# A Mamba and attention kernel: the convolution as four column strips over taps loaded from DRAM, residuals on TensorE, and 10 of 16 pairs on GpSimd

## The chip, the cores and the metric

The kernel runs on one core of a Trainium2 chip. The metric is the device time of one execution in microseconds; a time is the median of several runs. Besides that there is one profiled execution, with a record of every instruction on each engine: PE (TensorE), DVE (VectorE), ACT (ScalarE), POOL (GpSimd), and SP (SyncE), which only issues DMAs.

## The reference, cut to what matters

The input `x` is two images of 256 channels by 64 x 64 positions, that is 4096 tokens each, float32. Layer 0 is `x + mamba(groupnorm(x))`, layer 1 is `x + attention(groupnorm(x))`. The change lies in layer 0:

```python
yn = (y - mu) * lax.rsqrt(var + 1e-05) * gamma + beta        # layer norm over 256 channels
xz = yn @ W_in.T
xm, z = (xz[..., :DI], xz[..., DI:])                         # DI = 512
xc = lax.conv_general_dilated(xc, conv_w, ...)               # causal, 4 taps, each channel alone
u = jax.nn.silu(xc + conv_b[None, :, None]).transpose(0, 2, 1)
proj = u @ W_xp.T                                            # 16 + 16 + 16 columns
dt = jax.nn.softplus(proj[..., :R] @ W_dt.T + b_dt)
Bm = proj[..., R:R + N]
Cm = proj[..., R + N:]
def step(h, inp):                                            # over the 4096 tokens
    dA = jnp.exp(dt_t[:, :, None] * A)
    h = dA * h + (dt_t * u_t)[:, :, None] * B_t[:, None, :]
    return (h, jnp.einsum('bdn,bn->bd', h, C_t))
ym = (ys.transpose(1, 0, 2) + u * D) * jax.nn.silu(z)
y2 = ym @ W_out.T + yn
y3 = jax.nn.gelu(y2 @ W1.T + b1, approximate=False) @ W2.T + b2 + y2
```

Layer 1 is eight heads of softmax attention over the 4096 tokens of an image; the change doesn't touch its work.

## The kernel before, in words

`mamba_stage` does layer 0, `attention` layer 1, one after the other on the same core. Channels lie on the 128 partitions; tokens are cut into tiles of 512 (`T`), so there are 16 tiles, image 0's eight and then image 1's eight. For each tile there are three kinds of work:

- `front(i)` makes the layer norm, the convolution (`conv`, once for each of the `KD` = 4 blocks of 128 inner channels), the projection `W_xp`, and the softplus of `dt` (`softplus`, once a block). `dt` and `dt * u` are stored to DRAM, and the steps read them back four channels to a partition group, repeated (`load_rep`); B and C rows come back from DRAM broadcast over the partitions (`load_row`).
- `step(g)` is the recurrence. A tile has 32 steps: 4 channel blocks k, 4 groups of states, and two halves. A step has two exponentials on ACT (`da`, L853), a broadcast of B by PE into PSUM (`bn`), products with B, two scans on DVE (L869), and the product with C on POOL (L875, 1024 columns). Every second step, four matmuls with a 128 x 32 matrix of ones sum the states into four strips of 32 rows of `y` (L901). They need `bn`, `dtu_rep` and `dt_rep`; rings of five `h`, two `bn` and two `dbu` buffers lie between the engines.
- `back(i)` does `W_out`, the residual, the MLP with GELU, and the two last additions, takes the group-norm statistics and stores the tile. In image 1's time, `qkv` also makes image 0's queries, keys and values on PE.

A pair is two steps. `pooled(pair)` says whether the product of `dtu` with B for the pair's odd channels is made by POOL in one instruction (`both_times_b`, L864) or by DVE in two (`times_b(1)`, L860); the even channels are always DVE's.

The convolution before: PE projects a block into PSUM; ACT copies it behind three columns kept from the last tile (`xm`, L585 to L587, with `halo`); and PE adds up four matmuls, each with a diagonal matrix of one tap and with `xm` shifted by a column:

```python
matmul(pc.tile, [(taps[:, k, j, :], xm.tile[:, j : j + T]) for j in range(TAPS)])
```

An fp32 matmul shows as two records in the profile. The residuals before depend on the image. For image 0, PE adds them by matmuls with an identity matrix (L646, L684, L686) and ACT takes the sum out of PSUM (L660, L700). For image 1, DVE adds from PSUM (L663, L702).

The order of all this is written by a planner, `Plan`. Every `add(engine, due, cost, emit, reads, writes, tables, lands)` is one task. The planner runs a small model of the five engines with the stated costs; at each moment each engine takes, among the tasks that are ready, whose buffers are free and that are due no later than `HORIZON` after the oldest task not yet placed, the one with the lowest `due` (a task that needs another ACT table counts `SWITCH` later). Due times are in steps. The tasks are then emitted in that order, so each engine's instruction stream, SP's included, is fixed: an instruction that waits holds up all behind it on its engine. `front(i + 1)` is planned into the time of tile i's steps, `back(i)` into that of tile i + 1.

The prologue before the first scan holds loads of weights, the statistics of both images (`first`, L336 and L337), the group norm, and tile 0's whole front; image 1's tiles are loaded for their statistics into the `h` ring.

## Time and profile before

| | |
|---|---|
| Median of 3 runs | 4293.21 us (4290.18 to 4297.77) |
| Profiled execution | 4292.38 us, span 4290.6 us |
| PE busy | 4115.5 us, 96% |
| DVE busy | 3866.3 us, 90% |
| ACT busy | 3727.0 us, 87% |
| POOL busy | 3750.8 us, 87% |
| DMA | 389.58 MB, mean 91 GB/s |
| First and last scan | 81.5 and 1950.8 us |
| First matmul of attention | 1993.1 us |

A row of the groups of instructions reads: line, engine, operation, output from inputs by the program's names (PSUM tiles of the `mm` ring all show as `mm`), shapes, how many, then busy time and mean ns of one, then the idle time of the engine just ahead of them and what ended it. A row of the table of stretches reads: the stretch and its length, busy time (and instructions) of PE, PEld (weight loads), DVE, ACT and POOL, the granted TensorE clock, the share of DMA time and GB/s. A row of the timeline: start, length, engine, line and operation, count, and in brackets the idle time ahead. Busy PE time includes waits inside its pipeline, so it is an upper bound on its work.

### The profile page before, as it was taken

Reading aid. Unit: us, or ns where it says so; the run is one execution under the profiler, and the core shown is the slowest. Engines: PE = TensorE matmul, PEld = TensorE weight load, DVE = VectorE, ACT = ScalarE, POOL = GpSimd, SP = SyncE. Lnnn points to the kernel's source line nnn. Section 1 sums busy time; section 2 is a strip of 40 time slices with the busy share of each in tenths; the row PEclk is TensorE's granted clock in tenths of the full one; section 3 lists DMA queues with packets and bytes.
Section 4 is the critical chain, followed back from the end, with each engine's and each line's share of the span. In section 5 each row is a group of like instructions: output and inputs, shape, how many; then the busy total and the mean of one; then the engine's idle time right before and its main releaser. Section 6 shows DMA issues by size and latency. Waiting matters only on the chain.

```text
span 4290.6 us, 58937 instructions
## 1 busy us (share of the span) xinstructions
PE 4115.5 (96%) x21154; PEld 1799.6 (42%) x21154; DVE 3866.3 (90%) x3309; ACT 3727.0 (87%) x4982; POOL 3750.8 (87%) x1913
## 2 busy tenths in 40 slices
PE   6799999999999999988999999999999999999998
PEld 2233333333334333333444444444454444444443
DVE  5899999999999999995898989899858989898998
ACT  5789898998788888875999999999859999999997
POOL 3999999999899999994898888889728988888887
PEclk8899999999999999999999999999999999999999
DMA  6334333334444444447101040110182110401100
GB/s 212 107 114 130 117 115 123 128 128 133 150 146 160 162 141 140 143 166 167 33 18 28 18 106 18 28 30 21 50 253 54 32 28 18 106 22 25 29 21 9
DMA packets 172302, 389.58 MB, mean 91 GB/s; under 512 B 23392, under 2 KB 49760, under 8 KB 163808
## 3 DMA queue, kind: packets, MB, share of 16 engines
q1 hardware_dynamic: 171120, 383.37, 29.4%
q8 instruction: 168, 2.75, 0.3%
q10 hardware_dynamic: 880, 2.36, 0.3%
q14 instruction: 134, 1.10, 0.1%
HBM read 292.33 MB, written 93.32 MB: 90 GB/s over the span
## 4 chain that ended last, share of the span: by engine, by line
PE 79%; DVE 12%; ACT 4%; issue 3%; DMA 1%; POOL 1%; SPq 0%; DVEq 0%; POOLq 0%; ACTq 0%
PE s L1162 25%; PE po L1199 23%; PE mm L448 15%; DVE h L869 7%; PE mm L688 4%; PE y L901 4%; PE bn L448 2%; PE mm L647 2%; DVE bn L860 2%; ACT da L853 1%; PE s L1046 1%; PE y L899 1%; ACT L248 1%; PE sums_ps L1250 1%; PE mm L684 1%
## 5 line engine op out<-in xcount | busy, mean ns | idle before, releaser
L1184 DVE TENSOR_REDUCE chunk<-chunk 128x1024 f32<-128x4096 f32 x288 | 1269.8, 4409 | 176.4 <-ACT chunk L1175 174.7
L1232 POOL TENSOR_TENSOR acc_p<-acc_p,e 128x1024 f32<-128x1024 f32 x480 | 1167.3, 2432 | 124.1 <-ACT e L1175 99.4
L875 POOL TENSOR_TENSOR h<-h,c 128x1024 f32<-128x1024 f32 x512 | 1203.4, 2376 | 32.8 <-issue 15.7
L1175 ACT ACTIVATE e<-s 128x1024 f32<-128x1024 f32 x1056 | 1084.6, 1030 | 91.8 <-PE s L1162 56.7
L1162 PE MATMUL s<-q,k 128*128 128x512 f32 x4096 | 1155.8, 415 | 7.0 <-ACT chunk L1175 2.6
L1175 ACT ACTIVATE chunk<-s 128x1024 f32<-128x1024 f32 x992 | 1119.8, 1129 | 48.2 <-PE s L1162 22.9
L1199 PE MATMUL po<-chunk,v 128*32 128x512 f32 (+1 forms) x5248 | 1057.0, 521 | 0.0
L1199 PE MATMUL po<-e,v 128*32 128x512 f32 (+1 forms) x5504 | 1019.3, 500 | 1.5 <-ACT e L1175 1.5
L1162 PEld LDWEIGHTS s<-q,k 128*128 128x128 f32 x4096 | 714.3, 189 | 624.8 <-ACT e L1175 235.4
L853 ACT ACTIVATE da<-dt_rep,neg_a 128x512 f32<-128x512 f32 x1024 | 695.6, 702 | 105.8 <-DVE h L869 101.4
L1230 POOL TENSOR_TENSOR acc_p<-acc_p,e 128x512 f32<-128x512 f32 x480 | 621.8, 1295 | 94.7 <-ACT e L1175 64.8
L869 DVE TENSOR_TENSOR_SCAN h<-da,state,dbu 128x512 f32<-128x512 f32 x512 | 651.5, 1275 | 14.3 <-PE y L901 7.1
L869 DVE TENSOR_TENSOR_SCAN h<-da,state,bn 128x512 f32<-128x512 f32 x512 | 647.0, 1264 | 11.4 <-PE y L901 5.5
L864 POOL TENSOR_TENSOR dbu<-dtu_rep,b 128x1024 f32<-128x1024 f32 x176 | 417.8, 2374 | 17.0 <-issue 7.3
L448 PE MATMUL bn<-proj,pick 112*128 112x512 f32 x512 | 341.9, 669 | 87.9 <-DVE h L869 84.8
L248 ACT ACT_TABLE_LOAD x312 | 400.3, 1283 | 6.2 <-PEq L1502 0.7
L1199 PEld LDWEIGHTS po<-e,v 128*32 128x32 f32 x5504 | 251.8, 109 | 269.7 <-issue 104.4
L860 DVE TENSOR_TENSOR bn<-dtu_rep,bn 128x512 f32<-128x512 f32 x512 | 346.8, 680 | 16.8 <-PE bn L448 8.5
L1199 PEld LDWEIGHTS po<-chunk,v 128*32 128x32 f32 x5248 | 241.5, 108 | 250.7 <-issue 250.7
L1229 DVE TENSOR_TENSOR acc<-acc,e 128x512 f32<-128x512 f32 x448 | 309.6, 691 | 17.4 <-ACT chunk L1175 0.5
L901 PE MATMUL y<-h,sum 128*32 128x512 f32 x2048 | 302.0, 615 | 8.5 <-POOL h L875 8.3
L448 PE MATMUL mm<-yn,w_in 128*128 128x512 f32 x512 | 257.0, 627 | 8.2 <-ACT yn L538 3.6
(149 smaller groups left out, 4177.2 us busy)
## 6 DMA issues: line engine op xcount, KB each, us to landing
dt_rep<-dt_dram SPq DMA_DIRECT2D x128, 512.0 KB, 5.0
dtu_rep<-dtu_dram SPq DMA_DIRECT2D x128, 512.0 KB, 5.3
k<-qk_dram SPq DMA_DIRECT2D x62, 512.0 KB, 7.4
q<-qk_dram SPq DMA_DIRECT2D x124, 256.0 KB, 4.8
b<-bc_dram SPq DMA_DIRECT2D x64, 256.0 KB, 3.2
c<-bc_dram SPq DMA_DIRECT2D x64, 256.0 KB, 3.9
dt_dram<-dt SPq DMA_DIRECT2D x64, 256.0 KB, 2.2
dtu_dram<-lw SPq DMA_DIRECT2D x64, 256.0 KB, 3.7
```

Source lines behind the costliest of these rows:

```text
L248: self.nc.scalar.preload_act_table_set(self.TABLES[task.table])
L448: nc.tensor.matmul(out, lhsT=lhsT, rhs=rhs, start=(i == 0), stop=(i == len(pairs) - 1))
L853: nc.scalar.activation(da[j].tile, dt.tile[:, j, :], AF.Exp, scale=scale)
L869: nc.vector.tensor_tensor_scan(h.tile[:, j, :], da[j].tile, dbu, initial, ALU.mult, ALU.add)
L875: nc.gpsimd.tensor_tensor(h.tile, h.tile, rows_c.tile.unsqueeze(1).to_broadcast([P, 2, T]), ALU.mult)
L901: nc.tensor.matmul(y.tile[j * PQ : (j + 1) * PQ, :], lhsT=sum4, rhs=pair[j // 2].h.tile[:, j % 2, :], start=False, stop=(qd == NQ - 1),)
L1162: nc.tensor.matmul(ps[:, j, :], lhsT=keys[i // NT, kt][:, h, kj : kj + P], rhs=queries[i][:, h, :], start=True, stop=True)
L1175: nc.scalar.activation(e, todo[s].s[half], AF.Exp, scale=SCALE)
L1184: nc.vector.tensor_reduce(out, terms, AX.XY, ALU.add)
L1199: nc.tensor.matmul(tiles[i].po[h * D : (h + 1) * D, cols], lhsT=v[:, c, g * P + h * D : g * P + (h + 1) * D], rhs=todo[s].e[h // 2][:, h % ...
L1230: nc.gpsimd.tensor_add(acc_p[:, 1, :], acc_p[:, 1, :], eb[:, 1, :])
L1232: nc.gpsimd.tensor_add(acc_p, acc_p, eb)
```

## The change

Three things change in the Mamba stage, and with them the due times of nearly all tasks and `HORIZON` (28 to 32).

1. The convolution. The projected block is copied whole to `xm`, stored to a row in DRAM that holds the image's whole length with three zeros ahead (`rows_x`), and read back by four loads, one a tap j: the row shifted by j columns, 32 channels to a partition group, four groups of channels side by side. So partition 32 j + c of `xs` holds tap j of channel c of each group. Four matmuls then do the convolution, one for each group of 32 channels, with a 128 x 32 matrix that holds the taps, into four strips of 32 rows of one PSUM tile. The `halo` copies are gone; eight small stores zero the rows' first three columns. `xs` has one buffer; for tile 0 all blocks but k = 2 use the two `dtu_rep` buffers. `xm` has two buffers, not three.
2. The residuals of image 1 are made as those of image 0: identity matmuls on PE, eviction by ACT.
3. `pooled` gives POOL 10 of 16 pairs, not 11.

`range_t`, a small tile of the attention stage, is allocated after the Mamba stage. The attention stage's instructions are unchanged. Cut to its core (due times and the residual code of image 1 that merely goes are shortened):

```diff
-HORIZON = 28
+HORIZON = 32
...
-    r_xm = Ring(sc, [P, HALO + T], "xm", 3)
+    r_xm, r_xs = ring("xm", 2, pool=sc), ring("xs", 1, TAPS, pool=sc)
...
-        add("SP", due + 8, 0.8, load, [], [xt], lands=3.0)
+        add("SP", due + 2.5, 0.8, load, [], [xt], lands=3.0)
...
-    taps = wp.tile([P, KD, TAPS, P], F32, name="taps")
+    taps = wp.tile([P, KD, P // PQ, PQ], F32, name="taps")
     for k in range(KD):
-        for j in range(TAPS):
-            nc.vector.tensor_scalar_mul(taps[:, k, j, :], ident, conv_w[:, k, j : j + 1])
+        for g in range(P // PQ):
+            nc.vector.tensor_scalar_mul(taps[:, k, g, :], same, conv_w[:, k, g : g + 1])
...
-    halo = wp.tile([P, IMAGES, KD, HALO], F32, name="halo")
-    nc.vector.memset(halo, 0.0)
+    rows_x = [[dr.tile([P, HALO + L], F32, name="x_dram", bufs=IMAGES * KD) for _ in range(KD)] for _ in range(IMAGES)]
+    row_bufs = [[Buf(parts=NT) for _ in range(KD)] for _ in range(IMAGES)]
+    for x in itertools.chain(*rows_x):
+        nc.sync.dma_start(x[:, 0:HALO], state[:, 0, 0, 0, 0:HALO])
...
-        px, pc, xm = Buf(mm), Buf(mm), Buf(r_xm, 2)
-        h = halo_buf[b * KD + k]
+        px, pc, xm, xs = Buf(mm), Buf(mm), Buf(r_xm), Buf(r_dtur if d is tiles[0] and k != 2 else r_xs, TAPS)
+        at, row = t * T, row_bufs[b][k]
...
+        def store():
+            nc.sync.dma_start(rows_x[b][k][:, HALO + at : HALO + at + T], xm.tile)
+
+        def load(j):
+            src = rows_x[b][k][:, at + j : at + j + T].rearrange("(g c) t -> c g t", c=PQ)
+            nc.sync.dma_start(xs.tile[j * PQ : (j + 1) * PQ, :, :], src)
+
         def convolve():
-            matmul(pc.tile, [(taps[:, k, j, :], xm.tile[:, j : j + T]) for j in range(TAPS)])
+            for g in range(P // PQ):
+                matmul(pc.tile[g * PQ : (g + 1) * PQ, :], [(taps[:, k, g, :], xs.tile[:, g, :])])
...
-        add("ACT", due - 5, 0.15, lambda: nc.scalar.copy(xm.tile[:, 0:HALO], halo[:, b, k, :]), [h], [xm[0]])
-        add("ACT", due + 2, 0.49, lambda: nc.scalar.copy(xm.tile[:, HALO:], px.tile), [px], [xm[1]])
-        add("ACT", due + 4, 0.25, lambda: nc.scalar.copy(halo[:, b, k, :], xm.tile[:, T:]), [xm], [h])
-        add("PE", due + 4.5, 3.44, convolve, [xm], [pc, d.u[k]])
+        add("ACT", due + 2, 0.49, lambda: nc.scalar.copy(xm.tile, px.tile), [px], [xm])
+        add("SP", due + 7.5, 0.9, store, [xm], [row[t]], lands=2.0)
+        for j in range(0, TAPS, 2):
+            add("SP", due + 2, 1.7, lambda j=j: (load(j), load(j + 1)), [row[t], row[max(t - 1, 0)]], [xs[j], xs[j + 1]], lands=3.3)
+        add("PE", due + 4, 1.1, convolve, [xs], [pc, d.u[k]])
...
-                if k == 0 and b == 0:
+                if k == 0:
                     nc.tensor.matmul(po.tile, lhsT=ident, rhs=yn.tile[:, m, :], start=True, stop=False)
...
-            if b == 0:
-                keep = lambda m=m, po=po: nc.scalar.copy(yn.tile[:, m, :], po.tile)
-                add("ACT", due + 2 * m + 8.5, 0.49, keep, [po], [yn[m]])
-            else:
-                plus = lambda m=m, po=po: nc.vector.tensor_add(yn.tile[:, m, :], yn.tile[:, m, :], po.tile)
-                add("DVE", due + 2 * m - 1.5, 0.6, plus, [po], [yn[m]])
+            keep = lambda m=m, po=po: nc.scalar.copy(yn.tile[:, m, :], po.tile)
+            add("ACT", due + 2 * m + 7, 0.49, keep, [po], [yn[m]])
...
-                    if b == 0:
-                        nc.tensor.matmul(acc.tile, lhsT=ident, rhs=xt.tile[:, m, :], start=False, stop=False)
+                    nc.tensor.matmul(acc.tile, lhsT=ident, rhs=xt.tile[:, m, :], start=False, stop=False)
...
-                x = xt.tile[:, m, :]
-                if b == 0:
-                    nc.scalar.activation(x, acc.tile, AF.Identity, bias=b_2[:, m : m + 1])
-                else:
-                    nc.vector.scalar_tensor_tensor(x, acc.tile, b_2[:, m : m + 1], x, ALU.add, ALU.add)
+                nc.scalar.activation(xt.tile[:, m, :], acc.tile, AF.Identity, bias=b_2[:, m : m + 1])
...
-        return pair * 11 % 16 < 11
+        return pair * 10 % 16 < 10
...
-        add("SP", g - 5.5, 1.7, load, [src], [rep[at], rep[at + 1]], lands=3.3)
+        add("SP", g + 2.5, 1.7, load, [src], [rep[at], rep[at + 1]], lands=3.3)
...
-        add("DVE", g + 4, 0.6, lambda: times_b(0), [dtu[quarter]], [bn])
+        add("DVE", g + 12.5, 0.6, lambda: times_b(0), [dtu[quarter]], [bn])
         for j, dbu in ((1, dbu1[quarter // 2]), (0, bn)):
-            add("DVE", g + 5, 1.185, lambda j=j: scan(j), [da[j], dbu, state_buf[states[j]]], [h[j]])
+            add("DVE", g + 12.5, 1.185, lambda j=j: scan(j), [da[j], dbu, state_buf[states[j]]], [h[j]])
...
-    add("SP", -19.5, 2.4, load_late, [], [late_buf], lands=12.0)
+    add("SP", -22, 2.4, load_late, [], [late_buf], lands=12.0)
...
+    taps = given["L0_conv_conv_w"].reshape(-1, P // 32, 32, 4)
+    arrays["conv_taps"] = taps.transpose(3, 2, 0, 1).reshape(P, -1)
+    arrays["same"] = np.kron(np.ones((4, 1)), np.eye(32)).astype(np.float32)
```

## The prediction

> **What bounds the kernel now.** I read the table of stretches first, cut at tile boundaries: four whole tiles of the first image (from the first `L646` matmul of one tile to that of the fourth after it) and four of the second (by the first `L663` addition). Columns: length, then busy time of PE, PEld, DVE, ACT and POOL, granted clock, DMA share, GB/s.
>
> ```profile
> 439.27:899.82 460.55, 440.54 (x1394) 168.77 (x1393) 444.62 (x485) 414.98 (x717) 458.05 (x221) 1.00 0.39 124
> 1273.52:1742.84 469.32, 460.49 (x1490) 187.21 (x1489) 462.43 (x518) 414.41 (x725) 459.54 (x221) 1.00 0.46 155
> ```
>
> Per tile: image 0 takes 115.1 us, of which POOL is busy 114.5, DVE 111.2, ACT 103.7. Image 1 takes 117.3, with DVE 115.6, PE 115.1, POOL 114.9, ACT 103.6. So image 0 is POOL's, and in image 1 three engines are level. Attention (from about 1963 us) is not touched by the change; I carry it unchanged.
>
> Next, the groups of instructions by shape, for prices:
>
> ```profile
> L875 POOL TENSOR_TENSOR h<-h,c 128x1024 f32<-128x1024 f32 x512 | 1203.4, 2376 | 32.8 <-issue 15.7 <-ACT state L872 14.1 <-POOL h L875 2.3
> L864 POOL TENSOR_TENSOR dbu<-dtu_rep,b 128x1024 f32<-128x1024 f32 x176 | 417.8, 2374 | 17.0 <-issue 7.3 <-PE bn L448 4.6 <-DMA dtu_rep<-dtu_dram 2.3
> L860 DVE TENSOR_TENSOR dbu<-dtu_rep,bn 128x512 f32<-128x512 f32 x160 | 107.8, 675 | 9.3 <-PE bn L448 8.4
> L663 DVE TENSOR_TENSOR yn<-yn,mm 128x512 f32<-128x512 f32 x15 | 10.3, 686 | 3.1 <-PE mm L647 2.9
> L702 DVE SCALAR_TENSOR_TENSOR x_back<-mm,b,x_back 128x512 f32<-128x512 f32 x14 | 10.5, 747 | 2.6 <-PE mm L688 2.6
> ```
>
> Instructions overlap a little at their ends: four POOL products run 9.33 us back to back in the timeline, 2.33 each; the starts of consecutive DVE elementwise ones stand 0.60 apart. I use these net costs.
>
> The timeline then gives both forms of matmul, side by side, at full clock:
>
> ```profile
> 1300.00 1.07 PE L901 MATMUL y<-h,sum 128*32 128x512 f32 x8
> 1301.33 3.60 PE L448 MATMUL mm<-xm,taps 128*128 128x512 f32 x8
> ```
>
> Eight records (one fp32 matmul is two) take 0.99 us in the chain when they go to four column strips, and 3.44 (8 x 0.43) over the full width.
>
> Last, start and end: SP's timeline, PE's at the start, and PE after the last scan.
>
> ```profile
> 29.52 4.55 SPq L336 DMA_DIRECT2D h<-in_x  x5
> 40.24 3.08 SPq L336 DMA_DIRECT2D h<-in_x  x3
> ...
> 47.01 7.03 PE L448 MATMUL mm<-xm,taps 128*128 128x512 f32 x16
> 54.82 3.63 PE L448 MATMUL mm<-u,w_xp 128*48 128x512 f32 x8 [0.44 <-ACT u L582]
> ...
> 1962.74 14.08 PE L448 MATMUL mm<-yn,w 128*128 128x512 f32 x32
> 1976.66 1.02 PE L684 MATMUL mm<-yn,ident 128*128 128x512 f32 x2
> 1977.52 7.03 PE L688 MATMUL mm<-hid,w 128*128 128x512 f32 x16
> ```
>
> SP is still issuing bulk loads at 43.3; PE runs without a gap in the last tile's residual and MLP, up to attention's first matmul.
>
> **The skill.** The Trainium skill, TensorEngine Tiling (Array Packing), Theoretical Speedup, gives up to 4x for a side of 32; the two rows above agree (3.44 against 0.99, 3.5x). DMA: Bandwidth & Descriptors, Queues, rings and completion order, says that each DMA engine takes descriptors in ring order: a small store queues behind bulk loads issued before it. Loads of `h` in the first 50 us land after up to 12 us, median 6.7, which fits. SBUF — State Buffer, Who interferes with whom: a DVE instruction with two SBUF inputs blocks against a GpSimd one for its whole length. Here the 128x1 subtraction at 1085.18 lasts 5.59 us, until POOL falls idle at 1090.76. The operations that the change adds to DVE read PSUM and one SBUF tensor, so they don't meet this lock.
>
> **The change, part by part,** per tile unless said.
>
> 1. *Ten pairs of 16 on POOL.* POOL loses one `L864` product: -2.32. DVE gains two `L860` products: +1.2 to +1.35.
> 2. *Image 1's residuals.* DVE loses two `L663` and two `L702`: 2 x 0.60 + 2 x 0.67 = -2.55. PE gains four identity matmuls of 0.86: +3.44. ACT gains two copies (0.58) and two Identity evictions (0.68): +2.5.
> 3. *Convolution.* PE: 4 x (3.44 - 0.99) = -9.8. ACT loses eight copies of three columns (0.187): -1.5. SP gains 4 stores and 16 loads. At 0.33 (the row of `dt_dram`) and 0.33 to 0.53 (`b`) that is 6.6 to 9.8 us of issue, over the roughly 17 it has now. They move 20 x 256 KB = 5.2 MB: 124 GB/s becomes about 172 in image 0, 155 about 203 in image 1; DMA share from 0.39 and 0.46 to about 0.53 and 0.60. I count this as nothing in mid-stream: the convolution of the next tile is made while this one's 32 steps run, and `u` k=3 of it can't be written before this tile's k=2 begins (five `u` buffers), so a round trip of 6 to 9 us has a cover of tens of us. Without that cover it would cost 6 us four times a tile. The loads start at odd addresses; the worst I allow is a fifth more DMA time, still below 0.75 share.
>
> The sum: image 0 has POOL 112.2, DVE 112.4, PE 9.8 lighter. Image 1 has POOL 112.6, DVE 114.2 (115.6 - 2.55 + 1.2), PE 108.7, ACT 104.6. DVE becomes the bound everywhere, with POOL level in image 0. The busiest engine is at 99.5% of the period in image 0 today (one engine at the top) and 98.5% in image 1 (three near it). After, two near the top: I take 99%. Periods 113.5 and 115.4, gains 1.6 and 1.9. Ends: at 99.5% 2.1 and 2.5; at 98% 0.4 and 0.8. Times 8 tiles each: -13 and -15, together -28 (ends -10 and -37).
>
> 4. *Start.* The four convolutions now go through DRAM before `u` exists, and nothing else can run. Four `w_in` pairs end near 40, so a copy is ready from 36. But SP takes its queue in order, and the image-1 loads ahead of it stall for buffers to 40.24 and issue to 43.3. First store about 43.5, landing about 48 behind 1.5 MB; its four loads land about 52, then two to two and a half us for each further convolution: last one at 59, silu 60.5, against `w_xp` starting at 54.82 now. +6. Best case, with SP free at 36: last convolution at 50, -3. Worst, with the eight small stores that zero the halos (8 x 0.4 us of issue) ahead as well and full DMA engines: +12. The first scan starts at about 81 today and shifts by the same.
> 5. *End.* The last tile's four added identity matmuls lie on PE's gapless run after 1955: +3.4. Bounds 0 (if the first pair runs ahead of the last gate) to 4.
> 6. *Order.* Due times and HORIZON move everywhere; a common shift of an engine's due times changes no ranking on that engine. Priced at 0, bounds -10 (the stretch 1080 to 1120, where POOL idles 10.3 us of 40 around the group norm) to +10.
>
> Sum: -28 + 6 + 3.4 = about -19. The profiled execution took 4292.4 us, span 4290.6; its span goes to about 4272, its time to 4273.5, and the runs' median, 4293.2, lies 0.8 above that time: 4274.
>
> **The rivals.**
>
> *PE was the brake (more gain).* The chain of waits gives PE most of image 1 and half of image 0, and DVE waits on PE's `bn` and `y`. If the lighter PE lets DVE and POOL run at 99.5% (-37), the start costs only 2, and the image boundary recovers 5: about 4257. Against it: POOL at 99.5% of image 0 can't be explained by PE.
>
> *No change.* Two engines level at the top starve each other through five `h` and two `dbu` buffers: 98%, -10, and start plus tail give +9: 4292. For it: no stretch of this kernel shows two engines above 98.6%.
>
> *Slower: SP's queue.* Each convolution puts a wait for a store's landing (2.2 to 3.7 us in the rows of `dt_dram` and `dtu_dram`) at the head of SP's in-order queue; behind it stand the `dt_rep` and `dtu_rep` loads, for which ACT's exponentials and DVE's products wait. At 1 us of recurrence lost for each of the 60 convolutions after the first tile it is +60, less the 19: about 4334; at 0.5 us, 4304. It decides from 19/60, about 0.3 us per convolution. Against it: today DVE loses only 7.6 us to `dtu_rep` in the whole run, while SP already waits such landings out 84 times.
>
> *The convolution doesn't pack* (column strips don't overlap because each strip has its own weights): PE keeps 3.44, image 1's PE rises above 118 and binds: slower, but `y` also loads weights for every strip and packs. I give it 0.02, within the slower case.
>
> **How the numbers follow.** Forecast 0.50 (4262 to 4287), more gain 0.20 (4248 to 4262), no change 0.13 (4285 to 4300), slower 0.17 (above 4302, centred at 4312). The measurement tells about 0.2%, 8.6 us: faster means below 4284.6, slower above 4301.8. Faster: 0.47 + 0.20 + 0.01 = 0.68; same: 0.03 + 0.12 = 0.15; slower 0.17. The range leaves out half of the slower case and a little at the bottom: 4250 to 4306; the forecast's own is 4262 to 4287.
>
> **What would show it.** The convolution's matmuls take about 1 us for eight records; `L864` counts 160 and `L860` on `dbu` 192; no DVE row for image 1's residuals; tile periods near 113.5 and 115.4 with DVE the busiest; first scan near 87; PE's tail after the last gate 3.4 longer; DMA share near 0.53 and 0.60. Wrong if DVE waits show `dtu_rep` or ACT's show `dt_rep` for tens of us, if a period stays at 115 with DVE and POOL both under 98%, or if the first scan comes after 93.

## The result, and the profile after

The changed kernel takes 4336.1 us (median of 4 runs, 4332.2 to 4339.3) against 4292.8 for the kernel before on the same chip: a ratio of 1.0099, interval 1.0081 to 1.0116. It is slower by 1%, where I forecast 4274 and gave slower 0.17. The profiled execution has a span of 4337.5 us.

I divided both spans at the first `W_out` matmul of each tile, which stands once in every tile in both kernels. A tile's period is the time from one such matmul to the next. (The forecast's -28 us counted eight tiles of each image; the table has seven periods of image 0, so its column adds up to -17.)

| Stretch | Before | After | Difference | Predicted |
|---|---|---|---|---|
| span's start to tile 0's `W_out` | 209.8 | 251.9 | +42.1 | +6 |
| seven periods of image 0 | 807.7 (115.4 each) | 818.2 (116.9 each) | +10.6 | -11.2 (-1.6 each) |
| tile 7's `W_out` to tile 15's | 938.3 | 927.9 | -10.4 | -15.2 (-1.9 each) |
| tile 15's `W_out` to the end | 2334.8 | 2339.5 | +4.6 | +3.4 |
| span | 4290.6 | 4337.5 | +46.9 | -17 |

Two rows carry the miss: the start (36 us more than forecast) and image 0 (22 us more).

The engines' work came out as summed. This is the table of stretches of the changed kernel, four whole tiles of each image, with the same columns as before:

```profile
369.50:835.64 466.14, 417.60 (x1393) 153.13 (x1392) 445.60 (x493) 390.76 (x668) 450.53 (x217) 0.95 0.57 168
1310.08:1771.81 461.73, 440.52 (x1525) 172.80 (x1521) 456.42 (x510) 409.86 (x701) 450.50 (x218) 0.99 0.67 204
```

Per tile, image 0 has POOL 112.6 (forecast 112.2), DVE 111.4 (112.4), PE 104.4; image 1 has DVE 114.1 (114.2), POOL 112.6 (112.6), PE 110.1 (108.7). But image 0's tile takes 116.5 in this stretch, so no engine is above 96.7% of it. PE has 9.8 us a tile less to do by the sum, but its busy time fell only from 110.1 to 104.4: its granted clock is 0.95 here, where it was 1.00. DMA share is 0.57 and 0.67 where I had 0.53 and 0.60.

The groups of instructions of the changed kernel show the parts themselves (lines have moved: `L876` is the product with C, `L865` and `L861` are the products of `dtu` with B, `L452` is the helper that makes most matmuls):

```profile
L876 POOL TENSOR_TENSOR h<-h,c 128x1024 f32<-128x1024 f32 x512 | 1204.4, 2371 | 75.6 <-ACT state L873 32.5 <-issue 24.8 <-POOL h L876 7.9
L865 POOL TENSOR_TENSOR dbu<-dtu_rep,b 128x1024 f32<-128x1024 f32 x160 | 379.2, 2370 | 13.5 <-DMA dtu_rep<-dtu_dram 9.6 <-DVE h L870 3.9
...
L861 DVE TENSOR_TENSOR dbu<-dtu_rep,bn 128x512 f32<-128x512 f32 x192 | 129.0, 672 | 24.1 <-PE bn L452 23.8
L452 PE MATMUL mm<-xs,taps 128*32 128x512 f32 x488 | 68.6, 635 | 24.0 <-DMA xs<-x_dram 17.7 <-ACT da L854 2.3 <-issue 2.0
```

Counts are 160 and 192, as forecast. What was not forecast is in the idle columns: POOL now waits 75.6 us ahead of its products with C, where it waited 32.8, and DVE waits 24.1 us ahead of `dbu`, nearly all for PE's broadcast of B (`bn`), where it waited 9.3.

The start of the changed kernel, from the timelines of DVE, SP and PE (start, length, instruction, and in brackets the idle time before it and who ended it):

```profile
29.87 17.55 SPq L336 DMA_DIRECT2D h<-in_x  x8
42.16 1.29 DVE L337 BATCH_NORM_STATS2 stats_in<-h 128x6 f32<-128x512 f32 x2 [15.21 <-DMA h<-in_x]
43.36 1.27 DVE L521 TENSOR_TENSOR yn<-yn,mm 128x512 f32<-128x512 f32 x2
55.86 3.29 SPq L583 DMA_DIRECT2D x_dram<-xm  x2
59.25 7.43 SPq L587 DMA_DIRECT2D dtu_rep<-x_dram  x8
66.78 2.26 SPq L583 DMA_DIRECT2D x_dram<-xm  x2
76.10 2.01 SPq L587 DMA_DIRECT2D xs<-x_dram  x4
78.24 3.19 SPq L587 DMA_DIRECT2D dtu_rep<-x_dram  x4
88.73 1.93 PE L452 MATMUL mm<-dtu_rep,taps 128*32 128x512 f32 x8 [2.45 <-DMA dtu_rep<-x_dram]
93.04 3.63 PE L452 MATMUL mm<-u,w_xp 128*48 128x512 f32 x8
119.60 0.70 DVE L861 TENSOR_TENSOR bn<-dtu_rep,bn 128x512 f32<-128x512 f32 x1 [6.75 <-DMA dtu_rep<-dtu_dram]
```

Two things can be seen here. DVE's order puts two statistics of the second image ahead of tile 0's centring (`L521`), which then runs at 43.4; before, it ran at 23.6. And the four convolutions go through DRAM in two rounds, since `xm` has two buffers: store, wait, load, and once more. `w_xp` starts at 93.0 instead of 54.8, and the first product with B comes at 119.6 instead of 79.1. (Tile 0's tap blocks lie mostly in `dtu_rep` buffers; that is why `L587` shows both names.)

The end has the added identity products where they were expected, in PE's gapless run:

```profile
2022.16 1.02 PE L693 MATMUL mm<-yn,ident 128*128 128x512 f32 x2
2023.02 1.02 PE L694 MATMUL mm<-x_back,ident 128*128 128x512 f32 x2
```

### The profile page after: what moved, and what is told of

The parts are those of the page before. It is cut to its first block, busy times and chain, and to the rows that moved or that the text cites. A ratio compares the mean times of both kernels' runs of the same rounds, so it can differ in the third digit from the quotient of the medians.

```text
span 4337.5 us, 59404 instructions
## 1 busy us (share of the span) xinstructions
PE 4037.8 (93%) x21218; PEld 1740.9 (40%) x21218; DVE 3851.7 (89%) x3308; ACT 3673.6 (85%) x4842; POOL 3713.9 (86%) x1897
## 4 chain that ended last, share of the span: by engine, by line
PE 76%; DVE 8%; ACT 6%; DMA 4%; issue 4%; POOL 1%; SPq 1%; DVEq 0%; ACTq 0%; POOLq 0%
PE s L1163 24%; PE po L1200 23%; PE mm L452 12%; PE mm L696 4%; DVE h L870 4%; PE y L902 4%; PE bn L452 2%; PE mm L660 2%; ACT da L854 1%; DMA dtu_rep<-dtu_dram 1%; DVE bn L861 1%; DVE dbu L861 1%; ACT L248 1%; PE s L1047 1%; PE y L900 1%
## 5 line engine op out<-in xcount | busy, mean ns | idle before, releaser
L876 POOL TENSOR_TENSOR h<-h,c 128x1024 f32<-128x1024 f32 x512 | 1204.4, 2371 | 75.6 <-ACT state L873 32.5
L452 PE MATMUL bn<-proj,pick 112*128 112x512 f32 x512 | 335.1, 659 | 142.1 <-DVE h L870 139.4
L865 POOL TENSOR_TENSOR dbu<-dtu_rep,b 128x1024 f32<-128x1024 f32 x160 | 379.2, 2370 | 13.5 <-DMA dtu_rep<-dtu_dram 9.6
L861 DVE TENSOR_TENSOR bn<-dtu_rep,bn 128x512 f32<-128x512 f32 x512 | 344.9, 675 | 31.8 <-DMA dtu_rep<-dtu_dram 19.4
L452 PE MATMUL mm<-yn,w_in 128*128 128x512 f32 x512 | 279.3, 678 | 31.5 <-ACT yn L542 28.4
```

The lines of the kernel that those rows point to most:

```text
L452: nc.tensor.matmul(out, lhsT=lhsT, rhs=rhs, start=(i == 0), stop=(i == len(pairs) - 1))
L861: nc.vector.tensor_mul(out, dtu.tile[:, quarter + j, :], bn.tile)
L876: nc.gpsimd.tensor_tensor(h.tile, h.tile, rows_c.tile.unsqueeze(1).to_broadcast([P, 2, T]), ALU.mult)
```

## The experiments

There are eighteen kernels, in four groups. One thing has to be known first: the planner writes the whole order from the list of tasks. An edit of a task or a due time makes it write another order. Experiments that let it do so (three of group 1) measure the edit and a new order together, and group 4 measures a new order alone; the others keep the planned list and change only what is named. Each run's periods come from one profiled execution. I call a wait that comes back in every tile a hold, and the store of x to DRAM with the loads that bring it back the trip.

### 1. First edits

**Statistics later.** Planned anew.

```diff
-            add("DVE", due - 4.5, 0.7, lambda k=k: stats(k), ...)
+            add("DVE", due + 10, 0.7, lambda k=k: stats(k), ...)
```

> Edit: the changed kernel, with image 1's input statistics ranked on DVE behind tile 0's centring and scaling (as they stood in the kernel before). Theory A (the DVE queue: tile 0's centring stands behind two statistics whose data lands at 42 us) expects the centring at about 24 instead of 43.4 us, the first product with B at about 100 instead of 119.6, and the whole run 20 us shorter, 4316. Rival B (the start is bound by DMA: the bulk loads and the tap loads share one queue, so the stores of tile 0 land late whenever they are issued) expects the centring at 24 as well but the first product no earlier than 112, and the run at 4328. The stretches between the tiles' residual matmuls stay at 116.5 and 115.4 by both.

Measured: 4411.1 us, 1.0271 (1.0254 to 1.0288). The centring went back to 24.2, but `w_xp` only from 93.0 to 91.2 and the first product to 123.2. SP's timeline of this run says why:

```profile
34.83 8.74 SPq L336 DMA_DIRECT2D h<-in_x  x5
...
49.06 0.42 SPq L583 DMA_DIRECT2D x_dram<-xm  x1
...
56.09 6.46 SPq L587 DMA_DIRECT2D dtu_rep<-x_dram  x8
```

PE had made the first blocks at 30 to 40, yet the store is issued at 49: bulk loads of the second image, which wait for buffers, stand ahead of it in SP's queue. So the centring alone was not what bound the start. And the run is 75 us slower than the changed kernel, 67 of them from tile 7's `W_out` to tile 15's, where five tiles took 122 to 132 us. The new due time of 16 small instructions had changed the order of everything. Both theories missed by over 80 us.

**No trip through DRAM.** Stores and loads of x are gone and the strips multiply `xm` itself, so the convolution is left out of the result. Planned anew.

```diff
-                matmul(pc.tile[g * PQ : (g + 1) * PQ, :], [(taps[:, k, g, :], xs.tile[:, g, :])])
+                matmul(pc.tile[g * PQ : (g + 1) * PQ, :], [(taps[:, k, g, :], xm.tile)])
...
-        add("SP", due + 7.5, 0.9, store, [xm], [row[t]], lands=2.0)
-        for j in range(0, TAPS, 2):
-            add("SP", due + 2, 1.7, ...)
```

> Edit: the changed kernel without the stores and tap loads; the four column strips multiply the projected block itself, so the convolution is left out of the result while PE and ACT do the same instructions. Theory D (in mid-stream the tap loads, a megabyte a block, run ahead of the dtu_rep loads in the DMA rings and make DVE wait) expects image 0's period to fall from 116.5 to about 113.5, DMA waits of DVE gone, the start 15 to 18 us shorter, in all about 4298. Rival L (DVE and POOL, both near the top, and PE's order of tasks starve each other; DMA is innocent) expects the start to be shorter all the same but image 0's period to stay at 116 to 116.5, in all about 4320.

Measured: 4300.5 us, 1.0014 (1.0007 to 1.0020); first product at 85.6, image 0 at 115.0 a tile. Without the trip, and in a new order, the kernel is 36 us faster than the changed one: tile 0's `W_out` comes 40 us earlier, image 0 takes 13.5 us less and image 1 10 us more. How much of the two images' difference is the order can't be told. The time is near theory D's, the period between the two theories. But even with the trip gone the kernel is not faster than before, though POOL and PE have less to do in it, and DVE less in image 1.

**The kernel before with 10 of 16 pairs on POOL.** Planned anew.

```diff
-        return pair * 11 % 16 < 11
+        return pair * 10 % 16 < 10
```

> Edit: the kernel before, with 10 of 16 pairs on POOL and nothing else. By the sum of the prediction POOL falls from 114.5 to 112.2 and DVE rises to 112.4 in image 0, and in image 1 DVE rises to 116.9 with PE at 115. If two level engines can run at 99%, image 0's period goes from 115.1 to about 113.5 (-11 over seven periods) and image 1's from 117.3 to about 118.5 (+8): the run is the same within 5 us. If they starve each other (rival L), image 0 gains nothing or loses (115 to 116) and the run is 8 to 15 us slower than before.

Measured: 4348.3 us, 1.0130 (1.0113 to 1.0147). The start is as before (first product at 77.9); the tiles of image 0 alternate between 112.6 to 116.4 and 122.6 to 124.2, those of image 1 take 111.5 to 124.6. Both forecasts (within 5 us, or 8 to 15 slower) missed: it is 54 us slower, and what share of that is the new order can't be told from this run.

**Tap loads in the order 0, 2, 1, 3.** Every engine's order is that of the changed kernel; only which of the four loads is issued second and third differs.

```diff
-            ... (load(j), load(j + 1)) ...      # j = 0, 2
+            ... (load(j), load(j + 2)) ...      # j = 0, 1
```

> Edit: the changed kernel with the four tap loads of a block issued in the order 0, 2, 1, 3 in place of 0, 1, 2, 3, so that two neighbours in the queue write the two halves of the partitions and not one half; every instruction stands in the same place. If neighbouring loads into one half of the partitions share too few paths, a tap load lands in about 4 us instead of 5.8, the wait of DVE for dtu_rep shrinks and the run is 8 to 16 us shorter. If the bytes alone count, landing and time stay as they are, 4336.

Measured: 4328.4 us (4324.7 to 4330.3), 1.0082 (1.0065 to 1.0099), about 8 us less than the change. The median landing of an `xs` load fell only from 5.8 to 5.5 us (4 was expected), and DVE's waits for `dtu_rep` in four tiles of image 0 fell from 6.3 to 3.0. Tile 0's `W_out` comes 6.6 us earlier, and image 0 takes 116.0 a tile. Group 3 has a run with the old load order and that same period, so the 0.9 us in image 0 can't be put down to the load order.

### 2. Image 0: why 116.9 and not 113.5

In the changed kernel DVE's waits in those four tiles, longest first (who waited for whom, total, times, longest):

```profile
DVE dbu L861 <- PE bn L452: 7.6, 8, 2.1
DVE bn L861 <- DMA dtu_rep<-dtu_dram: 6.3, 4, 2.2
```

Each is in the main one hold a tile. In the tile from 486.5 the first stands at 578.1 (1.90 us) and the second at 531.0 (1.58 us). The second is for a `dtu_rep` load issued right behind four tap loads of the next tile, landing some 10 us after issue. The first is PE's queue: the layer norm's variance product waits for ACT's square, and the sums and the `bn` broadcast that DVE needs stand behind it.

**Small tap loads.** Outside tile 0 a tap load moves 1/32 of its bytes, so the convolution's data are left out; same order, same number of loads.

```diff
+            n = T if d is tiles[0] else T // 32
-            nc.sync.dma_start(xs.tile[j * PQ : (j + 1) * PQ, :, :], src)
+            nc.sync.dma_start(xs.tile[j * PQ : (j + 1) * PQ, :, 0:n], src[:, :, 0:n])
```

> Left out: outside tile 0 each of the tap loads moves 1/32 of its bytes, and the convolutions there multiply one constant tile, so the output's later tiles are not the convolution of the data. Every engine's instructions stand in the order of the changed kernel, the same number of loads is issued and waited for; only the bytes (about 4 MB of some 13 MB a tile) go. Theory D, the bytes are what costs image 0 its period (the 6 us landings of x, dtu_rep and the tap blocks under load): the waits for dtu_rep in DVE's row (6.3 us in four tiles) and for the xs blocks on PE (17.7 us) nearly go, image 0's period falls from 116.9 to 113.5-114.5, and with the last tile and image 1 a little shorter the whole comes to 4305-4318 us. Theory O, it is the order of the work on DVE, GpSimd and PE (one hold of about 2 us a tile where two engines wait for each other) and the number of issues on SP: period stays 116-117 and the time 4328-4337 us. The start's first product with B stays at 115-120 us under both.

**Image 0's residuals left out.** The three identity products of a tile go, each of two matmuls, together 5.2 us of PE; same order.

```diff
-                if k == 0:
+                if k == 0 and b:
                     nc.tensor.matmul(po.tile, lhsT=ident, rhs=yn.tile[:, m, :], start=True, stop=False)
...
-                if f == 0:
+                if f == 0 and b:
                     nc.tensor.matmul(acc.tile, lhsT=ident, rhs=yn.tile[:, m, :], start=True, stop=False)
```

> Left out: the first image's residuals (three identity products a tile, six matmul records, 5.2 us of TensorE a tile), so the first image's result lacks its residuals. Nothing else differs from the changed kernel, every engine keeps its order, the bytes stay. In image 0 of the changed kernel the trace without the bytes showed TensorE busy without a gap for some 70 us of a tile, and DVE waiting about 2.4 us a tile for the bn broadcasts behind it. Theory P (TensorE's crowded 70 us, in which out-projection, the two feed-forward products and the next tile's input products stand together, hold image 0 at about 116): the period falls by 1-2.4 us, to 114.5-116 with the bytes still there, and the time to 4320-4330. Theory O (the bytes and SP's landings alone): the period stays at 116.5-117, the time at 4332-4340.

**Both left out.**

> Left out: both of what the two runs before it left out (31/32 of the tap loads' bytes outside tile 0, and the first image's residual products). Theory P: with neither, image 0 runs at DVE's and GpSimd's own work, 113.0-114.2 us a tile, which is the period that was predicted; the time is 4320 less some 8 x 2 us, 4300-4310. If the period stays at 115.5-116 neither bytes nor TensorE is what holds image 0, and the order of DVE, ACT and GpSimd among themselves is left; time 4316-4322.

Measured:

| | Time | Ratio to before | Image 0's period |
|---|---|---|---|
| changed kernel | 4336.1 | 1.0099 (1.0081 to 1.0116) | 116.9 |
| small tap loads | 4320.4 | 1.0061 (1.0045 to 1.0078) | 115.9 |
| residuals out | 4336.6 | 1.0097 (1.0080 to 1.0114) | 116.6 |
| both | 4308.7 | 1.0032 (1.0020 to 1.0045) | 114.4 |

Against the changed kernel's 116.9, taking away either one alone gives at most 1 us a tile, both together 2.5. The first row needs care: group 3 has a run with image 0's work, bytes and order unchanged and a period of 116.0. So only the 1.5 us by which the run with both lies below that is clear, and the bytes alone (115.9) may be worth nothing. Without the bytes the waits for `dtu_rep` were gone, those for `bn` stayed (10.2 us in four tiles against 10.8), and smaller ones for POOL and `y` came up; without the residuals the waits for `bn` stayed as well (9.4), and one for `dtu_rep` grew to 4.3. A wait that goes makes room for another. The small loads' result lies between its two theories, and the run without residuals is where theory O had it. Theory P, with its fall to 114.5 to 116 by the residuals alone, was wrong there and nearly right in the run with both (114.4, forecast 113.0 to 114.2). The stretch of that run:

```profile
360.00:817.19 457.19, 397.72 (x1345) 143.16 (x1344) 444.74 (x493) 389.75 (x668) 449.98 (x217) 0.96 0.42 135
```

With PE at 87% and DMA at 0.42, DVE is busy 97.3% and POOL 98.4%. So even then neither reaches my 99%.

**One pair moved in the kernel before.** The first part of the change in image 0 only, without a new plan: in the kernel before, the product of one pair in sixteen goes from POOL to DVE, at the place of that pair's other DVE products.

```diff
+        moved = b == 0 and g // 2 % 16 == 15
         def both_times_b():
+            if moved:
+                return
...
-        add("DVE", g + 4, 0.6, lambda: times_b(0), [dtu[quarter]], [bn])
+        add("DVE", g + 4, 0.6, lambda: (odd_on_vector(), times_b(0)), [dtu[quarter]], [bn])
```

> The kernel before, planned with 11 of 16 pairs as it was; only in the first image one pair in sixteen (one GpSimd product, 2.32 us a tile) is done by two DVE products (1.2 us a tile) at the place of that pair's other products, so that every engine's order is kept otherwise. This is the first part of the change in image 0 alone without a new plan. If the first part is worth what its engine work says (GpSimd 114.5 to 112.2, DVE 111.2 to 112.4 us a tile), image 0's period goes from 115.4 to 113.2-114 and the time to 4280-4288. If GpSimd was no brake of image 0 (TensorE, or the hand-overs, are), the period stays at 115.2-116 and the time at 4291-4300. The same step with a new plan cost 54 us.

Measured: 4303.1 us, 1.0020 (1.0013 to 1.0027), image 0 at 117.7. The same four tiles in the kernel before and in this run, and POOL's largest wait here:

```profile
327.00:784.80 457.80, 438.44 (x1394) 168.64 (x1393) 443.15 (x485) 413.64 (x714) 455.87 (x219) 1.00 0.38 124
328.56:798.85 470.29, 442.91 (x1394) 171.38 (x1392) 449.42 (x493) 416.59 (x716) 450.41 (x217) 0.98 0.37 121
```

```profile
POOL h L888 <- ACT state L885: 14.4, 18, 2.0
```

POOL has lost the work I priced: 450.4 in four tiles where it had 455.9 in 458 us, and it stands idle 5 us a tile. The tile is longer by more than the 1.6 us that DVE gained, and both forecasts missed. POOL waits for ACT's copy of the states, which waits for DVE's scan. So with POOL's and DVE's work level, neither runs at 99%: here they are at 95.8% and 95.6%, and in the changed kernel at 96.7% and 95.6%. That the level work is the reason is argued, not shown: the moved product also stands at one fixed place in an order that was made with that product on POOL, and DVE's waits for `bn` grew from 3.6 to 8.3 us in these four tiles. No run has tried other places.

**Two swaps in the list.** The two holds by order, with all the work: a `dtu_rep` load right behind the next tile's tap loads goes ahead of them (20 places), and the sums and `bn` broadcasts right behind a variance product go ahead of it (34 places).

```diff
+        hoist(("dtu",), ("xs",))         # a task of the first kind moves ahead of those of the second
+        hoist(("y", "bn"), ("var",))     # that stand right before it on its engine
```

> The changed kernel with every task as it was and two local swaps in the planned list. On SP, a dtu_rep load that stood right behind the next tile's tap loads stands ahead of them (20 places). On TensorE, the sums and bn broadcasts that stood right behind the next tile's variance product (four records, 3.8 us, waiting for an ACT square) stand ahead of it (34 places). DVE, ACT and GpSimd keep their order; no work or byte is left out. Theory H (image 0 loses its period in two holds that come once a tile, 1.6 us for dtu_rep and 1.9 us for bn, and both are matters of order): both waits fall below 0.5 us, image 0's period goes from 116.9 to 114-115 as it did with the bytes and the residual products left out, and the time to 4313-4324. Theory V (volume: bytes and TensorE's work): the waits move to other places, the period stays above 116, the time at 4331-4340.

Measured: 4357.9 us, 1.0149 (1.0134 to 1.0165), image 0 at 118.4. The wait for `dtu_rep` is gone and the waits for `bn` are down to 1.1 us in four tiles, and a third hold stands in their place, DVE's scaling behind the variance that now comes later. Theory H missed; the waits moved, as theory V said, but the time is above its range too:

```profile
DVE yn L568 <- ACT mm L559: 14.9, 4, 4.4
```

**The first swap alone.** Without the second of those two lines.

> The changed kernel with the first of the two swaps alone: on SP, the dtu_rep load that stood right behind the next tile's tap loads stands ahead of them (20 places); every other engine keeps its order. In the run with both swaps the wait for dtu_rep was gone, and a new one of 4.4 us a tile stood before DVE's scaling, for the variance product that the second swap had put later. If the first swap is good in itself, DVE's waits for dtu_rep in four tiles of image 0 fall from 6.3 us to below 1, image 0's period goes from 116.9 to 115.3-116.2 as with the bytes left out (the bn hold stays), and the time to 4322-4332. If the order on SP is not what makes that hold, 4333-4340.

Measured: 4330.4 us, 1.0091 (1.0076 to 1.0107), image 0 at 115.9. DVE has no wait for `dtu_rep` left among its five longest in four tiles; its waits for `bn` are 10.0. This is the same period as with the bytes left out, as was expected. But the run "Second image behind tile 0's tap loads" of group 3, where only the order at the start differs, has 116.0 with 4.0 us of waits for `dtu_rep` in its four tiles. So the load's place in the queue is shown to make this wait, and what the wait costs is not shown: next to that run its removal gives 0.1 us a tile. In all, seven runs that change nothing in image 0 or only its tap and `dtu_rep` loads (their order, bytes or place) lie between 115.9 and 116.0. Why the changed kernel's own profile shows 116.9 stays open; two of its seven periods, of 118.4 and 118.8, hold most of the excess.

**TensorE kept busy.** For the other hold I looked at the variance product itself. The view of the instructions that use the program's tile `tmp` gives, for image 0, the count, then least, median and greatest ns of a record, then first and last start. The kernel before, and the changed one:

```profile
L448 PE MATMUL mm<-tmp,lnmat x24: 592/592/697, 414.4 to 991.2; 128*128 128x512 f32 x24
```

```profile
L452 PE MATMUL mm<-tmp,lnmat x24: 697/1062/1223, 338.4 to 925.7; 128*128 128x512 f32 x24
```

The same product takes nearly twice as long. In the tile from 486.5 PE's timeline, DVE's next wait for `bn`, and the table of stretches read:

```profile
569.80 0.80 PE L452 MATMUL bn<-proj,pick 112*128 112x512 f32 x1 [3.09 <-DVE h L870]
571.33 3.78 PE L452 MATMUL mm<-tmp,lnmat 128*128 128x512 f32 x4 [0.73 <-ACT tmp L524]
578.13 0.69 DVE L861 TENSOR_TENSOR dbu<-dtu_rep,bn 128x512 f32<-128x512 f32 x1 [1.90 <-PE bn L452]
```

```profile
569.56:576.39 6.83, 5.86 (x7) 2.14 (x7) 6.67 (x8) 6.74 (x12) 6.63 (x6) 0.50 0.24 78
```

The product stands behind a gap of 3.09 us on PE (a `bn` broadcast that waits for DVE) and one of 0.73. The granted clock is 0.50 from 569.56 to 576.39, and the four records take 3.78 us, where the kernel before has 1.98. The Trainium skill, TensorE: Matmul & The Clock Gate, What's actually happening, says that PE's clock drops to half after an idle window of about 3.4 us. Here the clock fell with a gap of 3.09. So the run above, with the `dtu_rep` load ahead, got 28 products whose result is overwritten: in seven of image 0's tiles three in the gap and one ahead of the variance product.

```diff
+        busy = lambda: nc.tensor.matmul(var.tile, lhsT=lnmat, rhs=yn.tile[:, 0, :], start=True, stop=True)
```

> The run with the dtu_rep load ahead, and on TensorE 28 added products whose result is overwritten: in seven of image 0's tiles, three ahead of the bn broadcast that stands before the next tile's variance product, and one ahead of that product (0.86 us each at full clock). No other engine changes. The clock records of the traces say that the kernel before has no half-clock stretch between 330 and 1000 us, the changed kernel has some 13 us of them a tile, from just after a 3.1 us gap on TensorE (the bn broadcast waits for DVE), and there the variance product takes 3.8 us instead of 2.0. Theory C (the lighter TensorE falls to half clock in that gap, and the doubled variance product is the bn hold): with the gap filled the product takes 2.0 us, DVE's waits for bn in four tiles fall from 10 us to 2-4, image 0's period from 115.9 to 114.0-114.8, the time from 4330 to 4317-4324, although TensorE does 3.4 us more a tile. Theory Q (the hold is TensorE's queue, whatever its clock): the added work makes it longer, period 116.5-119, time 4335-4355.

Measured: 4330.6 us, 1.0091 (1.0076 to 1.0106), image 0 at 114.9. The view of the product again:

```profile
L495 PE MATMUL mm<-tmp,lnmat x24: 591/592/593, 340.4 to 916.7; 128*128 128x512 f32 x24
```

The product is back at full clock, DVE's waits for `bn` in four tiles fell from 10.0 to 6.9 us, and image 0's period from 115.9 to 114.9, with more work on PE. That is theory C's mechanism, with a period just above its range and less of the waits gone than it said (2 to 4 us were to be left). The whole time did not fall: in this profiled execution tile 0's `W_out` came 3.3 us later and the second image's stretch was 4.0 longer than in the run without the products, though neither holds any of them. So the doubled product is shown to be the clock's work, and to cost up to 1 us a tile; the time does not show a gain. The lighter PE is not the whole reason either: the run without the trip has the same PE work in another order, and there the product takes 592 ns a record (median). The kernel before is at full clock from 330 us to 997.6, where it has one half-clock stretch of 3.4 us.

### 3. The start: why +42 and not +6

**Second image behind tile 0's tap loads.** Same list, except that up to the last of tile 0's tap loads the second image's loads, statistics and group norm stand behind it.

```diff
-        for task in self.order():
+        for task in kept + later + tasks[last + 1 :]:
```

> The changed kernel with the list of tasks as planned, except that up to tile 0's last tap load the second image's loads for statistics, its statistics and its group-norm steps are put behind that load; from there on every engine's order is as in the changed kernel. Theory M (the start is lost in two places: 20 us because tile 0's centring stands behind two statistics of the second image, 18 us in two store-and-load rounds through DRAM): centring returns from 43 to about 24 us, the stores start at about 44 instead of 56, the last convolution is at about 77 instead of 89; the eight loads for statistics then stand on SP's queue ahead of the B, C store, and DVE has 11 us of statistics behind them, so the first product with B comes at about 108 us instead of 119.6, and the time is 4322-4328. Theory B (SP's queue and the landings bound the start, as with the statistics moved in the plan): last convolution not before 85, first product 115-122, time 4331-4340.

Measured: 4340.2 us, 1.0117 (1.0100 to 1.0134), first product at 130.4. The centring is back at 23.7, as expected, but `w_xp` only starts at 102.9. Image 0, where every engine's order is the changed kernel's, takes 116.0 a tile, 0.9 less than there. In four of these tiles DVE still waits for `dtu_rep`:

```profile
DVE bn L870 <- DMA dtu_rep<-dtu_dram: 4.0, 4, 1.5
```

**And the stores ahead of the loads.** Blocks 2 and 3 are kept in a buffer that is idle at the start, so one round does for all four; taps in the order 0, 2, 1, 3.

```diff
+        own = xm_first[:, k - 2, :] if d is tiles[0] and k >= 2 else None
+        kept = kept[:first] + early + [task for task in kept[first:] if task not in early]
```

> As the run with the start unmixed, and tile 0's third and fourth stores to x_dram stand ahead of the first tap load on SP (their two chunks are kept in a buffer that is idle at the start), and each block's tap loads are issued in the order taps 0, 2, 1, 3 everywhere. Theory M: one round through DRAM in place of two: stores at about 40-45, sixteen loads issued one after the other at 0.93 us from about 50 to 65, last convolution at about 70, first product with B at about 100 us, and with the 8 us that the load order alone was worth the time is 4308-4316. Theory B: the loads and the bulk loads behind them take the same DMA time in whatever order, the first product at 110-118, time 4322-4330.

Measured: 4339.4 us, 1.0105 (1.0088 to 1.0122), first product at 129.4. The first product missed theory M's time by 22 us in the run before and by 29 here, for a reason of my own making: on PE and DVE the second image's group norm now stood ahead of tile 0's last convolutions. The tap loads were out at 67 us instead of 81, and then PE stood still until 88. Of the start they tell nothing against either theory.

**The group norm out of the way.** As before it, with the statistics behind tile 0's `w_xp` and the group norm behind the third softplus step. In names, each group behind the task ahead of it:

```diff
+        groups = [(before_loads, stores), (last_tap_load, bulk_loads), (w_xp_halves, statistics), (third_softplus, group_norm)]
```

> As the run with the start's stores first, but the second image's statistics stand behind tile 0's last w_xp step on DVE (its loads behind the last tap load on SP as there) and its group norm behind the third softplus step, so nothing of the second image stands ahead of tile 0's convolutions and w_xp. In the run with stores first, the tap loads were out at 67 us and TensorE then stood still from 66.7 to 88 us for the second image's group norm. Theory M: last convolution at 70-73, w_xp at 72-77 instead of 103, first product with B at 100-107 us instead of 129, time 4339 less 23-28, so 4311-4318. Theory B (landings and SP's queue, with the eight bulk loads ahead of the B and dt stores, bound it): w_xp before 80 but the first product not before 115, time 4322-4332.

Measured: 4323.6 us, 1.0072 (1.0055 to 1.0088); `w_xp` at 82.3 (theory M said 72 to 77), first product at 116.1 (100 to 107). Time and first product lie in theory B's ranges. Now nothing of the second image stands ahead of the trip. The first store is issued at 37.8 and lands 12.3 us later, and the last tap load lands at 77.2; SP's and PE's timelines and a stretch inside the trip show the rest:

```profile
50.07 8.75 SPq L613 DMA_DIRECT2D dtu_rep<-x_dram  x8
...
64.07 4.29 SPq L613 DMA_DIRECT2D dtu_rep<-x_dram  x4
...
82.27 3.63 PE L472 MATMUL mm<-u,w_xp 128*48 128x512 f32 x8
```

```profile
52.00:67.00 15.00, 5.18 (x20) 1.45 (x20) 0.00 (x0) 1.99 (x3) 0.00 (x0) 0.59 0.95 188
```

The same view of the kernel before, while the second image's bulk loads fill all 128 partitions:

```profile
31.00:44.00 13.00, 12.52 (x25) 5.44 (x26) 5.98 (x13) 5.66 (x13) 0.00 (x0) 0.87 1.05 386
```

With the DMA engines full in both, the tap loads move 188 GB/s and the bulk loads 386. Tile 0's sixteen tap loads, 4.2 MB, need 22 us at that rate, and their landings run from 55.6 to 77.2; to this comes the store's landing. The Trainium skill has this: SBUF — State Buffer, Door 1: The DMA port swizzle, says that a transfer's rate follows the number of SBUF ports its partitions reach, that 32 or 64 neighbouring partitions reach half of them, and gives 189 GB/s for 32 partitions and 328 for 128, measured at 1 MiB. The trace agrees in its 188; its 386 is above the page's 328, with several loads in flight. The page also says that +32 partitions stay on the same ports and +64 go to the other half. The gain of the load order 0, 2, 1, 3 points that way, but this run already has that order, and 188 is what it reaches with it. A rival is left: the tap loads also read rows that start at odd addresses, which the bulk loads don't, and no run here changes the one without the other.

**Tile 0's convolution direct.** The sorted start (the statistics now behind the first softplus step), both swaps, and in tile 0 the old convolution, from SBUF with sixteen 128x128 tap matrices in idle buffers.

```diff
         def convolve():
+            if d is tiles[0]:
+                matmul(pc.tile, [(wide[:, k, j, :], x_first[k][:, j : j + T]) for j in range(TAPS)])
+                return
```

> All in one: the sorted start, the tap loads in the order 0, 2, 1, 3, the two swaps of the run before it, and tile 0's convolution done from SBUF with sixteen 128x128 tap matrices as in the kernel before (in buffers that are idle at the start), so that no load stands between tile 0's input product and w_xp; tile 0's x is still stored for tile 1. The start should return to about that of the kernel before: w_xp at 55-60, first product with B at 80-90 us instead of 116 in the sorted start. If image 0 takes 114.5 a tile and image 1 115.3 as now, the time is 4336 less 34 for the start, 14 for image 0, and 0-3 for the loads' order: 4284-4292, at or just below the kernel before (4294). If the swaps don't help it is 4296-4304.

Measured: 4335.0 us, 1.0092 (1.0078 to 1.0106). `w_xp` is at 62.3, 20 us earlier than in the sorted start: that is the trip. The first product came only at 100.8, since SP's store of B and C stood until 76.7 behind a bulk load, and image 0 took 118.4, as with the two swaps. So the time missed what was expected by over 30 us.

**Direct, SP free, one swap.** Only the first swap, and the second image's statistics right behind tile 1's centring.

```diff
-        groups = [..., (first_softplus, statistics), ...]
+        groups = [..., (tile_1_centring, statistics), ...]
```

> The run with tile 0's convolution direct, without the second swap, and with the second image's statistics right behind tile 1's centring on DVE, so that SP is free of its bulk loads before tile 0's B, C store. In the run before, the store stood until 76.7 behind a bulk load that waited for a buffer. Expected: store at 64-68, first product with B at 86-93 us instead of 100.8 (and 119.6 in the changed kernel); image 0 at 115.5-116, image 1 at 115.3: 4336 less 28-33 for the start and 7-10 for image 0, so 4293-4301, level with the kernel before (4293) within what can be told. A result below 4285 would say that the convolution in mid-stream pays; one above 4305 that the start is still not what it was.

Measured: 4299.0 us (median of 21 runs), 1.0017 (1.0010 to 1.0023).

```profile
59.17 3.63 PE L509 MATMUL mm<-u,w_xp 128*48 128x512 f32 x8
63.99 0.33 SPq L629 DMA_DIRECT2D bc_dram<-bc  x1
...
90.95 0.69 DVE L942 TENSOR_TENSOR bn<-dtu_rep,bn 128x512 f32<-128x512 f32 x1
```

All of this is as expected. Against the kernel before, tile 0's `W_out` comes 11 us later, image 0 takes 4 us more, image 1 11 less, and the end 3 more. So 37 of the change's 43 us are gone, with all the work done: 31 of them at the start, and 7 in image 0, which has its 115.9 a tile.

**The same, with TensorE kept busy.**

> The run with tile 0's convolution direct, SP sorted and the dtu_rep load ahead (4299 us), with the same 28 added products on TensorE. Theory C: image 0's period from 115.9 to 114.0-114.8, the time 4285-4293, at or below the kernel before (4292.5). Theory Q: 4303-4325.

Measured: 4297.9 us (median of 13), 1.0008 (0.9999 to 1.0016), image 0 at 115.3, so 0.6 us less a tile than without the added products. Theory C missed, on the period and on the time. The variance product is at 592 ns again, but DVE's waits for `bn` in four tiles did not fall (10.6 us against 10.2): those ahead of `dbu` went from 9.6 to 5.6, and those ahead of the products into `bn` grew from 0.6 to 5.0. The run can't be told from the kernel before. No version here is faster than it.

### 4. The order by itself

**Planned anew, nothing else.**

```diff
-HORIZON = 32
+HORIZON = 31
```

> No work is changed: the planner's horizon is 31 instead of 32, which makes it choose another order. Theory R (a re-plan alone moves this kernel by tens of microseconds, since every due time was set against one order): at least 20 us from 4336, more likely slower, 4350-4410, and image 0's and image 1's periods scatter by 5 us or more from tile to tile. Theory S (the order is robust; what moved in the earlier runs was what their edits did): within 10 us, 4326-4346.

Measured: 4398.4 us, 1.0237 (1.0219 to 1.0254). Image 0's periods run from 115.3 to 122.2, image 1's from 115.9 to 136. Another order of the same work cost 62 us.

## Why the prediction was wrong, step by step

*Step 1, ten pairs of 16.* The engine work was right to 0.4 us for POOL and 1 us for DVE. The gain drawn from it was not: moving one pair at a fixed order made the tiles of image 0 in the kernel before longer by 2.3 us. The step behind it, "After, two near the top: I take 99%", failed in image 0. POOL ran at 99.5% as the only bound; in the changed kernel, with DVE level beside it, POOL ran at 96.7% and DVE at 95.6%. This fits the no-change rival, two level engines starving each other, and goes further than I let it (98%). That this is the reason, and not the place of the moved product, is not shown.

*Step 2, image 1's residuals on PE.* Right by the sum: DVE 114.1 a tile, forecast 114.2, and image 1's steady period about 115.4, forecast 115.4. Image 1 has DVE at 98.8% and PE's clock at 0.99, so 99% held there. No run has this part alone. The row of image 1 still gains 5 us less than forecast: its last two periods grew by 8.0 us (112.3 and 105.0 before, 116.9 and 108.4 after), which nothing here explains.

*Step 3, the convolution.* PE's part was right by the record (eight in about 1.1 us), but not its use. I took "PE 9.8 lighter" for slack, and durations for constant. In this order the lighter PE has a gap of 3.1 us a tile, its clock falls to half there, and the variance product behind it takes 1.8 us longer just where DVE waits for `bn`. With the gap filled, the period fell by 1.0 us in one pair of runs and 0.6 in the other. "I count this as nothing in mid-stream" was right for the convolution itself: the `xs` blocks cost PE 17.7 us in the whole run, 6.6 of them in tile 0. What I left out is that the tap loads delay others: median landings of `dtu_rep` rose from 5.3 to 6.6 us. That made one hold a tile in image 0, about 1.6 us of waiting, which goes when one load is put ahead; what it cost the period is not shown. My citation on ring order, a transfer queueing behind bulk loads issued earlier, fits this, and I drew no wait from it. DMA share was undersized by 0.04 to 0.07.

*Step 4, the start.* This step failed most: I forecast +6, bounds -3 to +12, and measured +42 at tile 0's `W_out` and +38 at `w_xp`. The largest term is the trip itself: leaving it out of tile 0 moved `w_xp` from 82.3 to 62.3. My "two to two and a half us for each further convolution" prices four loads of 256 KB at 420 GB/s or more; at the measured 188 they take 5.6 us, and the sixteen 22. The next term is order and rounds: sorting the start, with one round in place of two and the tap loads in their other order, took `w_xp` from 93.0 to 82.3. Two `xm` buffers make two rounds, and the second store's wait (66.8 to 76.1) was not in the sum; nor was the second image's work ahead of tile 0's. I did see the bulk loads in SP's queue and priced their issue, but took DVE's order from the kernel before. The centring's late place alone is not what cost the time: with it back at 24, `w_xp` came at 91.2 and 102.9. The last term is behind `w_xp`: with SP's bulk loads out of the way of the store of B and C, the first product came at 90.9 instead of 100.8.

*Step 5, the end.* I forecast +3.4 and measured +4.6. The added products stand where I put them, but the size can't be checked so finely: with the same end, the other runs in the planned order have 2335.1 to 2342.8 us for this stretch.

*Step 6, the order.* I wrote that "a common shift of an engine's due times changes no ranking on that engine. Priced at 0", with bounds of 10 us. This was wrong in kind: equal work in another order differed by 62 us. Two edits that let the planner run again came to 54 and 75 us, edit and order together. How much of the change's own +43 is its new order can't be told, since no run has the whole change in the old order.

*The rivals.* "Slower: SP's queue" gave 4334, and 4336 was measured, but that is luck: it priced a loss at each of 60 convolutions; what there was is a costlier start and one hold a tile in image 0. "PE was the brake" did not come true: with PE lighter, neither DVE nor POOL came above 96.7% in image 0. The convolution does pack.

What stays open: why image 0 has 116.9 in the changed kernel and 116.0 in the run where only the start differs; why level DVE and POOL stay below 99%; why the time of the run with TensorE kept busy did not follow its period; and whether another order of the changed kernel beats the kernel before.

## What to carry to other kernels

Price a load by a rate measured on loads of its own shape, and at the start of a kernel, where nothing covers it, by its whole bytes at that rate. When work is taken from a bound engine, ask who bounds next and what that engine's inputs wait for: its reachable share is its own, not the old bound's. An engine made lighter may get gaps and grow slower: read its durations again, not only its busy share. Where a planner or a hand-written order sets the queues, hold the order fixed to learn what a change does, since a new order alone may move the time by more than the change. And before a small gain is put down to an edit, look for a run that leaves that stretch alone: here one had the same 0.9 us.

## What was not expected of the hardware

TensorE's variance product went from 592 to 1062 ns a record in a kernel that gives TensorE less to do, and back to 592 when added products filled a gap of 3.1 us. Loads into 32 partitions, from rows at odd addresses, ran at 188 GB/s with the DMA engines 95% busy, against 386 for the bulk loads into 128. Issuing them so that neighbours in time lie 64 partitions apart went with 8 us of 4336. A wait for `dtu_rep` of 1.0 us a tile, in the run where only the start differs, was absent in the run with that load put ahead, and the period of image 0 went only from 116.0 to 115.9.
